# Moving the operands of a feed-forward network into an SBUF pool of their own, ahead of the others

## The chip, the core and the metric

The kernel runs on one core of a Trainium2 chip. The metric is the device time of one execution in microseconds (us). A profile of one execution gives, per instruction, its start and duration on each engine: TensorE (PE for matmuls, PEld for its weight loads), VectorE (DVE), ScalarE (ACT), GpSimd (POOL) and SyncE (SP), which issues the transfers.

## The reference

The input x is 4 x 1024 tokens of 512 features, fp32. It is layer-normalised to xn, and the output is x plus two branches of xn:

```python
# time mixing ("attention"), hidden width 704
xx  = shift_by_one_token(xn) - xn
k   = (xn + xx * time_mix_k) @ Wk.T
r   = (xn + xx * time_mix_r) @ Wr.T
state = state * w + relu(k_t)        # a scan over the tokens, w = exp(-exp(decay))
out = layernorm((state * r) @ Wv.T)
# feed-forward network (FFN), hidden width 2048
X = xn.astype(float16)
D = gelu(X.astype(float32) @ W0.T + bias0).astype(float16)
E = (D.astype(float32) @ W1.T + bias1).astype(float16)
```

## The kernel before

The tokens are worked in eight blocks of 512 (`blocks`, line 62). One pass of the loop at line 456 does for block i: the time mixing up to the gated states (`attention`), then the FFN (`ffn`), in which the other work of the block is placed between steps: `attention_out` ahead of step 0, the layer norm of the next block ahead of step 4, its transposes and mixed inputs ahead of step 7 (lines 478 to 481).

**Precision.** The products of the time mixing (lines 310, 345, 355) are fp32 matmuls, which the hardware records as two matmuls each. The FFN uses the type float32r, one matmul each; to keep its accuracy the weights are split into a high and a low part (`split`, line 115: ScalarE rounds, VectorE takes the difference), and both parts are multiplied into the same accumulator. The activations are fp16 values widened to float32r and need no split.

**The FFN.** Features lie on the 128 partitions. One step n of 16 covers 128 of the 2048 hidden units:

- *up* (`up`, lines 400 to 416): eight matmuls into one PSUM bank `pd`: for each of four feature chunks c, the stationary operand is a 128 x 128 piece of `w0h[c]` and then of `w0l[c]`, the moving operand `xf[:, c, :]` with 512 columns (line 405). ScalarE applies GELU to an fp16 tile `d16`, VectorE casts it to the float32r tile `d` (lines 413 and 415).
- *down* (`down`, lines 418 to 426): for each of four groups s of 128 tokens, the stationary operand is `d[:, s*128:(s+1)*128]`, the moving operand the high and then the low part of `w1` with 512 columns (line 420). The four accumulators `pe[s]` are kept over all 16 steps.

The up of step n + 2 is issued ahead of the down of step n (`AHEAD = 2`), so TensorE gets eight up matmuls, eight down matmuls, and so on; at the end of a block, where no up is left, the downs of steps 13, 14 and 15 follow one another, 24 in a row. In the last block those 24 are ordered by s (lines 442 to 447), so that each group of tokens can be finished early.

`w0h` and `w0l` are held in SBUF for the whole run. `w1` is too large for that: block 0 loads and splits it step by step and writes the parts to DRAM; later blocks read them back, 512 KB per step, into three buffers (`load_w1`, line 132). The two parts of the last step of the last block go to two buffers of the tag `raw` instead (lines 133 to 140).

**Where tiles lie.** `tile_pool` reserves SBUF for a pool when it is opened, pool after pool, and in a pool tag after tag in the order of first use, each tag with its number of buffers. So a tile's address follows from the sizes of all that stand ahead of it. The pools are `const` (one buffer for each name), `one`, `two`, `three` and `four` (lines 67 to 71), named after their number of buffers. `ident` (512 bytes per partition), small tables and the eight time-mixing weights of 2816 bytes stand first in `const`, so `w0h` and `w0l` begin at 896 modulo 2048 bytes, `xf`, which is in `one` behind `xnT` (8208 bytes) and others, at 992, and `w1` in `three` and `d` in `four` at 288.

Of the kernel before, what the change touches and what calls it, by code (L numbers as in the profile page):

```python
# [10 lines left out]
F32R = mybir.dt.float32r  # L11
# [3 lines left out]
P = 128  # L15
# [4 lines left out]
def time_mix_and_gelu_ffn(  # L20
# [27 lines left out]
    B, T, C = x.shape  # L48
    HID = wkT.shape[1]
    N = w0T.shape[1]  # L50
    TB = 512
    NS = TB // P
    NC = C // P
# [10 lines left out]
    def pool(name, bufs, **kw):  # L64
        return ctx.enter_context(tc.tile_pool(name=name, bufs=bufs, **kw))

    const = pool("const", 1)
    one = pool("one", 1)
    two = pool("two", 2)
    three = pool("three", 3)  # L70
    four = pool("four", 4)
# [43 lines left out]
    def split(hi, lo, raw):  # L115
        nc.scalar.copy(hi, raw)
        nc.vector.tensor_sub(lo, raw, hi.bitcast(F32))  # L117

    W0G = 512
    w0h = [const.tile([P, N], F32R, name=f"w0h_{c}") for c in range(NC)]  # L120
    w0l = [const.tile([P, N], F32R, name=f"w0l_{c}") for c in range(NC)]

    w1_dram = [dram.tile([P, 2, C], F32R, name=f"w1d_{n}") for n in range(NN)]

# [7 lines left out]
    def load_w1(i, n):  # L132
        if i == len(blocks) - 1 and n == NN - 1:

            parts = [
                three.tile([P, C], F32R, tag="raw", name=f"w1_{i}_{n}_{p}") for p in range(2)
            ]
            for p in range(2):
                nc.sync.dma_start(parts[p].bitcast(F32), w1_dram[n][:, p, :].bitcast(F32))
            return parts  # L140
        w1 = three.tile([P, 2, C], F32R, tag="w1", name=f"w1_{i}_{n}")
        if i == 0:
            raw = three.tile([P, C], F32, tag="raw", name=f"w1raw_{n}")
            nc.sync.dma_start(raw, w1T[n * P : (n + 1) * P, :])
            split(w1[:, 0, :], w1[:, 1, :], raw)
            nc.sync.dma_start(w1_dram[n].bitcast(F32), w1.bitcast(F32))
        else:
            nc.sync.dma_start(w1.bitcast(F32), w1_dram[n].bitcast(F32))
        return [w1[:, p, :] for p in range(2)]
# [128 lines left out]
        return x16s, xk  # L278

    def ffn_input(i, x16s):  # L280
        xf = one.tile([P, NC, TB], F32R, tag="xf", name=f"xf_{i}")
        for c in range(NC):
            nc.vector.tensor_copy(xf[:, c, :], x16s[c])
        return xf
# [103 lines left out]
    def finish(i, s, z, pe):  # L388
        b, t0 = blocks[i]
        e16 = two.tile([P, C], F16, tag="e16", name=f"e16_{i}_{s}")  # L390
        nc.vector.tensor_add(e16, pe, b1_sb)  # L391
        nc.vector.tensor_add(z, z, e16)  # L392
        nc.sync.dma_start(out[b, t0 + s * P : t0 + (s + 1) * P, :], z)

    def ffn(i, xf, between, state):


        pe = [ps_e.tile([P, C], F32, tag="pe", name=f"pe_{i}_{s}") for s in range(NS)]

        def up(n):  # L400
            pd = ps_mm.tile([P, TB], F32, tag="mm", name=f"pd_{i}_{n}")
            cols = slice(n * P, (n + 1) * P)
            for c in range(NC):
                for w in (w0h, w0l):
                    nc.tensor.matmul(  # L405
                        pd,
                        w[c][:, cols],
                        xf[:, c, :],
                        start=(c == 0 and w is w0h),
                        stop=(c == NC - 1 and w is w0l),  # L410
                    )
            d16 = two.tile([P, TB], F16, tag="d16", name=f"d16_{i}_{n}")
            nc.scalar.activation(d16, pd, AF.Gelu, bias=b0_sb[:, n : n + 1])  # L413
            d = four.tile([P, TB], F32R, tag="d", name=f"d_{i}_{n}")
            nc.vector.tensor_copy(d, d16)  # L415
            return d

        def down(n, s, d, w1):
            for part in range(2):
                nc.tensor.matmul(  # L420
                    pe[s],
                    d[:, s * P : (s + 1) * P],
                    w1[part],
                    start=(n == 0 and part == 0),
                    stop=(n == NN - 1 and part == 1),
                )

        last = 3 if i == len(blocks) - 1 else 0  # L430
        AHEAD = 2
        waiting = [(up(n), load_w1(i, n)) for n in range(AHEAD)]
        for n in range(NN):
            if n in between:
                between[n]()
            if n + AHEAD < NN:
                waiting.append((up(n + AHEAD), load_w1(i, n + AHEAD)))
            if n < NN - last:
                operands = waiting.pop(0)
                for s in range(NS):  # L440
                    down(n, s, *operands)
        if last:
            with tc.manual_schedule(engines={nc.tensor.engine, nc.vector.engine}):
                for s in range(NS):
                    for n, operands in zip(range(NN - last, NN), waiting):
                        down(n, s, *operands)
                    finish(i, s, state["zs"][s], pe[s])
        return pe
# [4 lines left out]
    nc.scalar.activation(w_sb, w_sb, AF.Exp)  # L453
    nc.scalar.activation(w_sb, w_sb, AF.Exp, scale=-1.0)
    xf = ffn_input(0, x16s)
    for i in range(len(blocks)):
        more = i + 1 < len(blocks)
# [25 lines left out]
        if more:  # L483
            x16s, xk = state["mixed"]
            xf = ffn_input(i + 1, x16s)
            for s in range(NS):
                finish(i, s, state["zs"][s], pe[s])
# [43 lines left out]
```

## Time and profile before

957.68 us, median of three runs (957.37 to 958.03); the profiled execution has a span of 956.5 us.

| view of the profile | what it says |
|---|---|
| TensorE clock granted | 0.998 of full on average; half speed only in the first microseconds and at the very end |
| pd matmuls, line 405 | 1024, mean duration 402 ns (with w0h) and 395 ns (with w0l) |
| pe matmuls, line 420 | 1024, mean duration 393 ns |
| weight loads of both | 188 ns each |
| fp32 matmuls, lines 310 and 345 | 960 of full size, mean 591 to 599 ns |
| GELU on ScalarE, line 413 | 128, 687 ns each |
| cast to d on VectorE, line 415 | 128, 424 ns each |
| w1 read back from DRAM | 111 transfers of 512 KB, 3.3 us from issue to landing (median) |
| DMA | 106.47 MB, 111 GB/s over the span |

A matmul's recorded duration reaches from its start to a modelled end, and the next one starts well before that end; the distance from start to start is what a matmul costs a busy TensorE. A group's line gives its merged busy time and the mean duration of one.

### The profile page before, as it was taken

What the parts mean: (1) busy time and instruction counts of PE and PEld (TensorE: products, weight loads), DVE (VectorE), ACT (ScalarE), POOL (GpSimd) and SP (SyncE); (2) the same over time, 40 slices, a digit from 0 to 9 for tenths busy, and PEclk for the clock granted to TensorE, in tenths of its full rate; (3) what the DMA queues carried; (4) which work ended last, traced back from release to release, by engine and by line L of the source; (5) the groups of instructions that cost most, each with busy time, mean ns of one, the idle gap of its engine ahead of it and who ended that gap; (6) DMA issues with size and microseconds to landing.
All of it is one profiled execution on the core that took longest, in us unless ns stands there. A gap on an engine that the chain in (4) does not pass through costs nothing.

```text
span 956.5 us, 8658 instructions
## 1 busy us (share of the span) xinstructions
PE 939.8 (98%) x3216; PEld 582.2 (61%) x3216; DVE 486.0 (51%) x836; ACT 160.5 (17%) x264; POOL 53.7 (6%) x128
## 2 busy tenths in 40 slices
PE   5999999999999999999999999999999999999998
PEld 2447764478644785458854488545884458744686
DVE  6548852385424844259343593436924279232512
ACT  5322320012100121002201021010210102101021
POOL 1001000010001000011000100001100020000100
PEclk9999999999999999999999999999999999999999
DMA  8734570045400354014530154302542023410243
GB/s 267 244 128 143 207 266 1 0 132 197 156 0 23 132 182 149 0 31 144 178 132 1 33 173 169 110 1 64 181 153 88 0 86 135 156 64 0 73 147 110
DMA packets 43368, 106.47 MB, mean 111 GB/s; under 512 B 8256, under 2 KB 8256, under 8 KB 43328
## 3 DMA queue, kind: packets, MB, share of 16 engines
q1 hardware_dynamic: 43328, 105.94, 33.0%
q8 instruction: 25, 0.41, 0.2%
q14 instruction: 15, 0.12, 0.0%
HBM read 89.14 MB, written 16.78 MB: 111 GB/s over the span
## 4 chain that ended last, share of the span: by engine, by line
PE 95%; DVE 3%; ACT 1%; DMA 0%; issue 0%; POOL 0%; SPq 0%; DVEq 0%
PE pd L405 24%; PE pe L420 23%; PE po L345 15%; PE pr L310 14%; PE pk L310 14%; PE pkr L310 3%; PE po L355 2%; DVE xnT L196 1%; DMA x<-in_L_attn_x 0%; DVE z L392 0%; DVE w L117 0%; DVE e L391 0%; DVE xk L275 0%; ACT xk L235 0%; DVE d L415 0%
## 5 line engine op out<-in xcount | busy, mean ns | idle before, releaser
L420 PE MATMUL pe<-w,d 128*128 128x512 f32 x1024 | 254.9, 393 | 0.9 <-DVE w L117 0.6
L420 PEld LDWEIGHTS pe<-w,d 128*128 128x128 f32 x1024 | 192.0, 188 | 45.1 <-DVE w L117 1.0
L405 PE MATMUL pd<-xf,w0h 128*128 128x512 f32 x512 | 205.8, 402 | 0.0
L405 PE MATMUL pd<-xf,w0l 128*128 128x512 f32 x512 | 202.0, 395 | 0.0
L413 ACT ACTIVATE d<-pd,b_sb 128x512 f16<-128x512 f32 x128 | 87.9, 687 | 428.8 <-PE pd L405 428.8
L310 PE MATMUL pk<-xk,wk 128*128 128x512 f32 x320 | 146.0, 599 | 3.1 <-DVE xk L242 3.1
L310 PE MATMUL pr<-xnT,wr 128*128 128x512 f32 x320 | 144.0, 591 | 0.0
L345 PE MATMUL po<-wv_sb,g 128*128 128x512 f32 x320 | 140.8, 595 | 0.0
L415 DVE CAST d<-d 128x512 fp32r<-128x512 f16 x128 | 54.3, 424 | 138.1 <-ACT d L413 137.2
L405 PEld LDWEIGHTS pd<-xf,w0h 128*128 128x128 f32 x512 | 96.1, 188 | 31.0 <-issue 5.9
L405 PEld LDWEIGHTS pd<-xf,w0l 128*128 128x128 f32 x512 | 96.1, 188 | 24.5 <-issue 1.9
L310 PEld LDWEIGHTS pk<-xk,wk 128*128 128x128 f32 x320 | 60.8, 191 | 78.5 <-issue 71.1
L310 PEld LDWEIGHTS pr<-xnT,wr 128*128 128x128 f32 x320 | 60.6, 189 | 76.9 <-issue 76.4
L345 PEld LDWEIGHTS po<-wv_sb,g 128*128 128x128 f32 x320 | 60.1, 190 | 75.6 <-issue 74.9
L196 DVE STREAM_TRANSPOSE xnT<-x 32x512 f32<-32x512 f32 x112 | 78.7, 703 | 2.2
L297 DVE TENSOR_TENSOR_SCAN st<-w_sb,carry,rk 128x512 f32<-128x512 f32 (+1 forms) x24 | 30.8, 1283 | 70.3 <-ACT rk L295 70.3
L295 ACT ACTIVATE rk<-pk 128x512 f32<-128x512 f32 x40 | 24.0, 601 | 233.3 <-PE pk L310 233.3
L175 DVE BATCH_NORM_STATS2 sty<-po 128x6 f32<-128x512 f32 x32 | 22.1, 689 | 72.8 <-PE po L355 67.9
L297 DVE TENSOR_TENSOR_SCAN st<-w_sb,rk 128x512 f32<-128x512 f32 (+1 forms) x24 | 29.3, 1222 | 54.9 <-ACT rk L295 54.8
L321 DVE TENSOR_TENSOR g<-st,pr 128x512 f32<-128x512 f32 x40 | 27.5, 687 | 53.7 <-PE pr L310 53.6
L169 POOL TENSOR_SCALAR ry<-mvy 128x1 f32<-128x1 f32 x32 | 11.4, 356 | 508.0 <-DVE mvy L176 508.0
L310 PE MATMUL pkr<-xnT,wr 128*64 128x512 f32 x64 | 29.2, 598 | 0.0
(56 smaller groups left out, 439.7 us busy)
## 6 DMA issues: line engine op xcount, KB each, us to landing
w<-w1d SPq DMA_DIRECT2D x111, 512.0 KB, 3.3
x<-in_L_attn_x SPq DMA_DIRECT2D x32, 256.0 KB, 4.3
xres<-in_L_attn_x SPq DMA_DIRECT2D x32, 256.0 KB, 2.7
w1d<-w SPq DMA_DIRECT2D x16, 512.0 KB, 3.3
out<-z SPq DMA_DIRECT2D x32, 256.0 KB, 4.8
w0raw<-in_L_ffn_W SPq DMA_DIRECT2D x16, 256.0 KB, 4.1
w1raw<-in_L_ffn_W SPq DMA_DIRECT2D x16, 256.0 KB, 4.0
wk<-in_L_attn_Wk SPq DMA_DIRECT2D x4, 352.0 KB, 6.2
```

The source lines that it names most:

```text
L175: nc.vector.bn_stats(st6, src)
L196: nc.vector.transpose(dst[i * Q : (i + 1) * Q, :, :, j, :], src[j * Q : (j + 1) * Q, :, :, i, :],)
L295: nc.scalar.activation(rk[:hw], pk, AF.Relu)
L297: nc.vector.tensor_tensor_scan(st[:hw], w_sb[:hw, h : h + 1].to_broadcast([hw, TB]), rk[:hw], 0.0 if t0 == 0 else carry[:hw, h : h + 1], A ...
L310: nc.tensor.matmul(dst, w[c][:, cols], src, start=(c == 0), stop=(c == NC - 1))
L321: nc.vector.tensor_mul(g[:, h, :], st, pr)
L345: nc.tensor.matmul(pos[s], g[:, h, s * P : (s + 1) * P], wv_sb[:, h, :], start=(first and h == 0), stop=(not first and h == NF - 1),)
L355: nc.tensor.matmul(pos[s], gh[rows, s // 2, :], wv_sb[rows, NF, :], start=first, stop=not first)
L405: nc.tensor.matmul(pd, w[c][:, cols], xf[:, c, :], start=(c == 0 and w is w0h), stop=(c == NC - 1 and w is w0l),)
L413: nc.scalar.activation(d16, pd, AF.Gelu, bias=b0_sb[:, n : n + 1])
L415: nc.vector.tensor_copy(d, d16)
L420: nc.tensor.matmul(pe[s], d[:, s * P : (s + 1) * P], w1[part], start=(n == 0 and part == 0), stop=(n == NN - 1 and part == 1),)
```

## The change

A pool named `wide` is opened ahead of all others. `w0h`, `w0l`, `xf`, `w1` (three buffers, as before) and `d` (four, as before) are allocated in it. All of them have buffers of 2048, 4096 or 8192 bytes per partition, so that each begins at the same offset modulo 2048.

```diff
+    wide = pool("wide", 1)
     const = pool("const", 1)
     one = pool("one", 1)
...
-    w0h = [const.tile([P, N], F32R, name=f"w0h_{c}") for c in range(NC)]
-    w0l = [const.tile([P, N], F32R, name=f"w0l_{c}") for c in range(NC)]
+    w0h = [wide.tile([P, N], F32R, name=f"w0h_{c}") for c in range(NC)]
+    w0l = [wide.tile([P, N], F32R, name=f"w0l_{c}") for c in range(NC)]
...
-        w1 = three.tile([P, 2, C], F32R, tag="w1", name=f"w1_{i}_{n}")
+        w1 = wide.tile([P, 2, C], F32R, tag="w1", name=f"w1_{i}_{n}", bufs=3)
...
-        xf = one.tile([P, NC, TB], F32R, tag="xf", name=f"xf_{i}")
+        xf = wide.tile([P, NC, TB], F32R, tag="xf", name=f"xf_{i}")
...
-            d = four.tile([P, TB], F32R, tag="d", name=f"d_{i}_{n}")
+            d = wide.tile([P, TB], F32R, tag="d", name=f"d_{i}_{n}", bufs=4)
```

The start addresses in the two built programs, modulo 2048 bytes (the pieces of one tile follow at multiples of 512 or 2048):

| tile | role | before | after |
|---|---|---|---|
| w0h, w0l | stationary, up | 896 | 128 |
| xf | moving, up | 992 | 128 |
| d | stationary, down | 288 | 128 |
| w1 | moving, down | 288 | 128 |
| raw (last step of the last block) | moving, down | 288 | 288 |
| all others (wk, wr, wv, xnT, xk, g, x, z, ...) | | as listed by the pools | the same offsets as before |

## The prediction

> **What bounds the kernel now.** I read the page from the top: busy shares, the chain of waits, the groups, and then, because a busy TensorE says little by itself, the timeline of single matmuls. The first two (busy line, then the chain by engine and by line):
>
> ```profile
> PE 939.8 (98%) x3216; PEld 582.2 (61%) x3216; DVE 486.0 (51%) x836; ACT 160.5 (17%) x264; POOL 53.7 (6%) x128
> ...
> PE 95%; DVE 3%; ACT 1%; DMA 0%; issue 0%; POOL 0%; SPq 0%; DVEq 0%
> PE pd L405 24%; PE pe L420 23%; PE po L345 15%; PE pr L310 14%; PE pk L310 14%; PE pkr L310 3%; PE po L355 2%; DVE xnT L196 1%; DMA x<-in_L_attn_x 0%; DVE z L392 0%; DVE w L117 0%; DVE e L391 0%; DVE xk L275 0%; ACT xk L235 0%; DVE d L415 0%
> ```
>
> TensorE carries 95% of the chain; the FFN's two products (pd and pe) are 47% of the span. Does it wait? All waits of TensorE:
>
> ```profile
> PE pt L223 <- DVE x L179: 8.3, 1, 8.3
> PE pk L310 <- DVE xk L242: 3.1, 2, 2.7
> PE pe L420 <- DVE w L117: 0.6, 1, 0.6
> PE pe L420 <- DVE d L415: 0.3, 1, 0.3
> ```
>
> 12.3 us in all, 11.4 of them at the start. So the time is the sum of the spacings between matmul starts, and only those can change it. The timeline of TensorE in block 2 (start, merged duration, group):
>
> ```profile
> 354.99 2.01 PE L420 MATMUL pe<-w,d 128*128 128x512 f32 x8
> 356.84 0.39 PE L405 MATMUL pd<-xf,w0h 128*128 128x512 f32 x1
> ...
> 358.70 2.01 PE L420 MATMUL pe<-w,d 128*128 128x512 f32 x8
> ...
> 362.41 5.65 PE L420 MATMUL pe<-w,d 128*128 128x512 f32 x24
> 367.90 2.31 PE L310 MATMUL pk<-xk,wk 128*128 128x512 f32 x5
> ```
>
> Eight pe take 356.84 - 354.99 = 1.85 us (231 ns each), eight pd 1.86 us (232.5 ns). Durations near 393 ns overlap and are not the rate. The last line pair is the important one: at a block's end there is no pd left and 24 pe stand in a row, 5.49 us, 229 ns each. Within that row the spacing settles. Its weight loads from the eleventh or so on, and a row of pd ahead of the attention output, where 16 pd stand together:
>
> ```profile
> 364.95 2.68 PEld L420 LDWEIGHTS pe<-w,d 128*128 128x128 f32 x12
> ```
>
> ```profile
> 290.98 0.39 PE L405 MATMUL pd<-xf,w0l 128*128 128x512 f32 x1
> ...
> 292.38 0.39 PE L405 MATMUL pd<-xf,w0l 128*128 128x512 f32 x1
> ```
>
> Twelve loads in 2.68 us, the last one 0.19 us long: (2.68 - 0.19) / 11 = 226.4 ns. From the 1 ns start times behind this view the settled pe spacing is 226, 227, 227 and again, 226.67 on average, in all eight blocks, from about the eleventh matmul on. The pd never get there: six intervals in 292.38 - 290.98 = 1.40 us are 233.3 ns, and the starts behind it read 238, 231, 231 (or 237, 231, 232) over and over. Settled, the same instruction on the same shapes costs 226.7 ns in pe and 233.3 ns in pd. In the eight-by-eight alternation that fills a block neither settles: pe repeats 229, 229, 233, 236, 224, 231, 236, 232. Over the kernel, leaving out the gaps over 300 ns, 1000 pd gaps average 232.46 ns and 1012 pe gaps 230.69 ns.
>
> **Why two rates: the addresses.** The products are alike in type, width and weight size. In pe the moving w1 starts at 288 modulo 2048 and the stationary d at 288 plus a multiple of 512: their distance is 0 modulo 512. In pd the moving xf starts at 992, the stationary w0 at 896 plus a multiple of 512: the distance is 416 modulo 512. Within pd four different w0 offsets (384, 896, 1408, 1920 modulo 2048) give one pattern, and within pe the four d offsets give one settled rate, so multiples of 512 don't matter here. The accumulation bank doesn't either: in the last block six pe in a row go to one bank, elsewhere two, and both settle at 226.67. What is left is how the stream of moving data and the weight load of the next matmul, which starts 3 ns after each matmul, lie to each other in SBUF. This is inferred from two configurations only; distance and absolute offset are not separated by the trace.
>
> **What the Trainium skill says.** "TensorE: Matmul & The Clock Gate", section "Step-by-step: what each phase is for": TensorE has two independent SBUF read ports, and loading the next weights doesn't steal bandwidth from the running matmul. The trace does not bear that out for this type: the fp32 products, where the load has time to spare, run at 429 ns for two passes, 214.5 a pass, and the one-pass products at 227 to 233. The same page, "Back-to-back issue gap", gives N/2.4 + 2.5, an estimate of 215.8 ns for 512 columns: the fp32 pass agrees, the FFN is 11 to 17 ns above it. "SBUF — State Buffer", "Specifications (TRN2)", gives 16-byte lines with a penalty on crossing. A 512-byte weight row has 32 of them, and 226.67 - 213.3 is 32 cycles at 2.4 GHz, 233.3 - 213.3 is 48: an estimate that fits, no more. The section "Operand start alignment" there speaks of legality and says that nothing was timed.
>
> **The change part by part.** *Instructions.* None is added, removed or moved: each engine's list, with its waits, is the same in both kernels, so no new wait and no new queueing. Cost 0, not even hidden work. *The other tiles.* The new pool is 94,208 bytes, 46 times 2048, so what stays behind it (wk, wr, wv, xnT, xk, g, x, d16, z) keeps its offset modulo 2048. I cost the attention's 1,152 fp32 matmuls and all of VectorE and ScalarE at nothing: same offset, and the other engines lie beside TensorE in any case. *The up product.* xf moves from 992 to 128, w0 from 896 to 128: distance 0 modulo 512. *The down product.* w1 and d both go from 288 to 128: distance unchanged. Also the change from one product to the other, every eight matmuls, now keeps the distance (before: weights 288 under xf 992, weights 896 under w1 288), so a settled stream need not be upset nearly 30 times a block.
>
> If distance decides, all settle at 226.67:
> - pd: 1000 x (232.46 - 226.67) = 5.8 us
> - pe: 1012 x (230.69 - 226.67) = 4.1 us
> - given back, settling: a stream that starts anew takes some ten matmuls. In the last block, after a 338 ns gap, 229, 233, 236, 224, 231, 236, 228, 233, 231 add up to 41 ns over the settled rate. Two new starts a block (after the attention, after its output) and one more in the last: 17 x 0.041 = 0.7 us.
> - given back, the last w1: its two parts lie in the pool of the raw loads, still at 288, against a d at 128. 24 matmuls in the last block alternate with it; at 4 ns each 0.1 us.
> - given back, block 0: its pe wait for the w1 split on VectorE (0.6 us above). The 168 FFN matmuls ahead of that wait would save about 168 x 4.9 ns = 0.8 us, which can be lost in it: between 0 and 0.8, taken as 0.4 since some of the loads may be early.
>
> Sum 9.9 - 0.7 - 0.1 - 0.4 = 8.7 us: 957.7 - 8.7 = 949.0 us. Faster TensorE makes no other engine the bound: a step of 16 matmuls shrinks from 3.71 to 3.63 us, while its w1 transfer lands in 3.3 us with three buffers, and one GELU (687 ns) and one cast (424 ns) are two steps ahead.
>
> **Rivals.**
> - *Absolute offset decides, the other way.* w0 is the operand on a multiple of 128 now, and pd is the slower product. If weights on such a border are what costs, pe joins pd at 233.3: 1000 x 0.87 + 1012 x 2.64 = 3.5 us, 961.2 us. For it: only two configurations are seen. Against: four w0 and four d offsets made no difference.
> - *The alternation never settles.* The pattern may come from the switching of products (a new accumulation, its semaphore), not from addresses. Then pd looks like pe now: 1000 x (232.46 - 231) = 1.5 us, 956.2 us; or nothing moves, 957.7. Against: the 24 pe in a row switch operands and accumulators too and stay settled.
> - *A clean border removes the whole overhead.* 128 is a multiple of 128 and 288 isn't. At the fp32 pass rate: 1000 x 17.96 + 1012 x 16.19 = 34 us, 923 us. Nothing seen runs so, with the load under a one-pass matmul.
>
> **Chances.** Distance decides 0.64; never settles or no change 0.12; absolute offset, slower 0.17; whole overhead gone 0.07. Faster by over 0.2% is 0.64 + 0.07 = 0.71, within 0.2% is 0.12, slower 0.17. The range: the first case with its unknowns (block 0 and settling, 947.8 to 950) widened to 945 for a rate a few ns better, and up to 959 over the no-change case and the near half of the slower one.
>
> **What would show it.** Right: pd and pe both at 226.67 away from new starts, eight of each in 1.81 us instead of 1.86 and 1.85; mean matmul durations of both groups near 389 to 390; fp32 rows at 592 as now; the same four waits of TensorE. Wrong: settled pd at 233, or a settled pe that is no longer 226.67 (then the absolute offset counts), or a longer wait for the w1 split in block 0 that eats the gain.

## The result, and the profile after

The changed kernel takes 949.54 us (median of six runs, 949.0 to 950.27) against 957.61 us for the kernel before in the same session (957.27 to 958.03): a ratio of 0.9916, 95% interval 0.9903 to 0.9928, or 8.1 us less. The two profiled executions lie further apart, 956.5 and 947.2 us: 0.9 us of that is TensorE's first wait, for x, which was 8.3 and 7.4 us long in them (7.2 to 8.5 us in the profiles of this document).

The busy line of the changed kernel's page and its chain by engine:

```profile
PE 931.0 (98%) x3216; PEld 583.0 (62%) x3216; DVE 485.7 (51%) x836; ACT 160.5 (17%) x264; POOL 53.7 (6%) x128
...
PE 93%; DVE 4%; ACT 1%; issue 1%; DMA 0%; POOL 0%; DVEq 0%
```

TensorE is as full as before and its busy time is 8.8 us shorter with the same 3216 instructions; no other engine's busy time moved by more than 0.8 us. All waits of TensorE in the changed kernel:

```profile
PE pt L226 <- DVE x L182: 7.4, 1, 7.4
PE pk L313 <- DVE xk L245: 3.1, 2, 2.8
PE pe L423 <- DVE w L120: 0.8, 1, 0.8
PE pe L423 <- DVE d L418: 0.6, 2, 0.3
```

The same four lines; the two in front of pe grew from 0.9 to 1.4 us. The wait for w stands in block 0 in both kernels. The one wait for d of before stands in the last block and is still there; the second, 0.30 us, is new and stands in block 0 as well. The timeline of TensorE in block 2 (start, merged duration, group), at the place that was shown of before:

```profile
351.49 1.98 PE L423 MATMUL pe<-w,d 128*128 128x512 f32 x8
353.30 0.39 PE L408 MATMUL pd<-xf,w0h 128*128 128x512 f32 x1
...
355.11 1.98 PE L423 MATMUL pe<-w,d 128*128 128x512 f32 x8
...
358.74 5.60 PE L423 MATMUL pe<-w,d 128*128 128x512 f32 x24
364.18 3.17 PE L313 MATMUL pk<-xk,wk 128*128 128x512 f32 x7
```

Eight pe take 353.30 - 351.49 = 1.81 us and eight pd 355.11 - 353.30 = 1.81 us (before 1.85 and 1.86), 226.7 ns each by the 1 ns start times behind this view. The row of 24 takes 5.44 us instead of 5.49, 226.7 ns from its first matmul on. In the starts the alternation reads 226, 227, 227 in pd, in pe, and across every switch.

What is left shows after a new start. The first pd after block 2's attention, in the same view:

```profile
286.99 0.40 PE L408 MATMUL pd<-xf,w0l 128*128 128x512 f32 x1
...
289.31 0.39 PE L408 MATMUL pd<-xf,w0l 128*128 128x512 f32 x1
289.54 0.39 PE L408 MATMUL pd<-xf,w0h 128*128 128x512 f32 x1
...
290.45 4.02 PE L348 MATMUL po<-wv_sb,g 128*128 128x512 f32 x9
```

Ten intervals in 289.31 - 286.99 = 2.32 us are 232 ns each; the next four read 226, 227, 227 and 226 in the starts. Before, this row stayed at 233.

The sum over the kernel, from the starts (gaps over 300 ns left out again; a gap counts for the product it starts in, up to the next FFN matmul):

| | before, ns | after, ns | us |
|---|---|---|---|
| pd, 1000 gaps (999 after) | 232.46 | 227.43 | -5.0 |
| pe, 1012 gaps | 230.69 | 226.87 | -3.9 |
| gaps over 300 ns of block 0's FFN, beyond what ordinary gaps take | | | +0.75 |
| all fp32 matmuls | 463.84 us | 463.80 us | 0.0 |

-8.9 + 0.75 is -8.15 us; the medians differ by 8.1.

### The profile page after: what moved, and what is told of

Its sections match the earlier page's. It is cut to its first block, busy times and chain, and to the rows that moved or that the text cites. A ratio compares the mean times of both kernels' runs of the same rounds, so it can differ in the third digit from the quotient of the medians.

```text
span 947.2 us, 8658 instructions
## 1 busy us (share of the span) xinstructions
PE 931.0 (98%) x3216; PEld 583.0 (62%) x3216; DVE 485.7 (51%) x836; ACT 160.5 (17%) x264; POOL 53.7 (6%) x128
## 4 chain that ended last, share of the span: by engine, by line
PE 93%; DVE 4%; ACT 1%; issue 1%; DMA 0%; POOL 0%; DVEq 0%
PE pd L408 23%; PE pe L423 22%; PE po L348 15%; PE pr L313 15%; PE pk L313 14%; PE pkr L313 3%; PE po L358 2%; DVE xnT L199 1%; DVE w L120 1%; DVE stx L178 0%; DVE d L418 0%; DMA x<-in_L_attn_x 0%; DVE z L395 0%; DVE e L394 0%; DVE xk L278 0%
## 5 line engine op out<-in xcount | busy, mean ns | idle before, releaser
L423 PE MATMUL pe<-w,d 128*128 128x512 f32 x1024 | 251.2, 390 | 1.4 <-DVE w L120 0.8
L408 PE MATMUL pd<-xf,w0l 128*128 128x512 f32 x512 | 199.9, 390 | 0.0
```

The lines of the kernel that those rows point to most:

```text
L408: nc.tensor.matmul(pd, w[c][:, cols], xf[:, c, :], start=(c == 0 and w is w0h), stop=(c == NC - 1 and w is w0l),)
L423: nc.tensor.matmul(pe[s], d[:, s * P : (s + 1) * P], w1[part], start=(n == 0 and part == 0), stop=(n == NN - 1 and part == 1),)
```

## The experiments

The distance theory was that the settled spacing of float32r matmuls depends on the distance between moving operand and weights. Its rivals were that the absolute offset decides, and that the switch from one product to the other does, wherever the operands lie.

### Distances and offsets by themselves

```diff
+    for r, (m, d) in enumerate(runs):            # 45 pairs (moving offset, distance), bytes
+        m, w = m // 4, (4096 + m + d) // 4
...
+        for k in range(REP):      # 64
+            nc.tensor.matmul(q, big[:, w : w + P], big[:, m : m + 512], ...)
```

> The kernel leaves the model out altogether: 45 rows of 64 float32r matmuls (128 x 128 weights, 512 columns) on one tile, each row with its own offset of the moving operand and its own distance to the weights; the output is not the reference's. Rows a to aa..bf: moving operand at a multiple of 2048 bytes, distance 0, 16, 32, ... 496 bytes beyond 4096; then distances 512, 1024, 1536, 4 and 8; then distance 0 with both operands moved by 16, 32, 64, 160, 256, 288; then distance 416 with both moved by 32 and 96. Distance theory: distance 0 settles at 226.7 ns, also when both are moved and at 512, 1024 and 1536; distance 416 settles at 233.3 ns, also when both are moved; other distances lie between or beyond. Absolute-offset theory: the rows with both operands moved differ from the row at the same distance by several ns. If switching of products and not addresses made the difference, all 45 rows settle alike.

(By the kernel's own comment `big` begins at a multiple of 512 bytes; that it is one of 2048, as the text says, is not shown. No distance depends on it.)

Some rows of its timeline (start, merged duration; a row's 64 matmuls cost the difference between its start and the next row's). qab is distance 16, qac 32, qad 48; qaq 256, qar 272, qas 288, qat 304:

```profile
22.71 14.68 PE L70 MATMUL qab<-big 128*128 128x512 f32 x64
37.23 15.09 PE L70 MATMUL qac<-big 128*128 128x512 f32 x64
52.15 15.09 PE L70 MATMUL qad<-big 128*128 128x512 f32 x64
...
245.24 14.67 PE L70 MATMUL qaq<-big 128*128 128x512 f32 x64
259.75 14.68 PE L70 MATMUL qar<-big 128*128 128x512 f32 x64
274.26 15.09 PE L70 MATMUL qas<-big 128*128 128x512 f32 x64
289.19 15.09 PE L70 MATMUL qat<-big 128*128 128x512 f32 x64
```

14.52 us at 16, 14.92 at 32; 14.51 at 256 and 272, 14.93 at 288: the pattern returns after 256 bytes. Settled spacings (second half of each row):

| distance, bytes | ns | distance, bytes | ns |
|---|---|---|---|
| 0 | 226.7 | 128 | 233.5 |
| 16 | 226.7 | 144 | 233.5 |
| 32 | 233.4 | 160 | 233.4 |
| 48 | 233.3 | 176 | 230.0 |
| 64 | 233.2 | 192 | 228.9 |
| 80 | 232.0 | 208 | 231.9 |
| 96 | 234.3 | 224 | 233.3 |
| 112 | 233.3 | 240 | 226.7 |

The rows 256 to 496 repeat these within 0.1 ns, and 512, 1024 and 1536 give 226.7. With both operands moved by 32, 64, 160, 256 or 288 bytes distance 0 stays at 226.7, and 416 stays at 233.3 when both are moved by 32 or 96. So with the moving operand on a 32-byte border and distances in steps of 16 bytes, the distance modulo 256 decides, and 226.7 ns is the least that any distance gave. Distances 4 and 8 cost 232.5 and 230.6. Off the border the rule fails: with both operands moved by 16, distance 0 costs 231.1. All FFN tiles of these kernels begin at multiples of 32.

### All operands together, elsewhere

```diff
     wide = pool("wide", 1)
+    shift = wide.tile([P, 40], F32, name="shift")    # 160 bytes ahead; another pool behind
+    nc.vector.memset(shift, 0.0)                     # keeps the other tiles where they were
...
```

> All FFN operands together at 288 modulo 2048 instead of 128, all other tiles where they were. Distance theory: as the changed kernel, 949.5 us within 0.5, all float32r matmuls settled at 226.7 ns. Absolute-offset theory: w0 leaves its multiple of 128 bytes, so the time differs from 949.5 us by more than 1 us, in either direction.

949.36 us, 0.9908 of before (0.9895 to 0.9922). The average spacings are 227.04 ns in pd and 226.72 in pe: the multiple of 128 has no part in the settled rate. Both are a little under the changed kernel's. The last w1, which stays at 288, agrees with the rest here. And the first pd after the attention settle sooner: from block 1 on after four gaps (236, 228, 234, 230 in block 2, 21 ns over the settled rate together), where the changed kernel takes ten and 60 ns. So a new start depends on more than the distance, here by some 0.4 us over the kernel; on what is not known.

### The old distance at the new place

```diff
...
-        xf = wide.tile([P, NC, TB], F32R, tag="xf", name=f"xf_{i}")
+        xf = late.tile([P, NC, TB], F32R, tag="xf", name=f"xf_{i}")   # behind the other four and 96 bytes
```

> The changed kernel with only xf moved on by 96 bytes (224 against weights at 128), which is the old distance of the up product, 416 modulo 512, at the new place; all other tiles keep their offsets. Distance theory: pd settles at 233.3 ns again, pe is disturbed again by each switch, 957 to 958 us. Absolute-offset theory (weights and w1 stay where they are): 949.5 us.

959.1 us, 1.0012 of before (1.0006 to 1.0019): moving one tile by 96 bytes takes all of the gain away, and 1 us more than I had expected. The first groups of its page answer to those of the changed kernel, which follow:

```profile
L430 PE MATMUL pe<-w,d 128*128 128x512 f32 x1024 | 254.3, 393 | 1.0 <-DVE w L123 0.6 <-DVE d L425 0.3
L415 PE MATMUL pd<-xf,w0h 128*128 128x512 f32 x512 | 207.6, 406 | 0.0
L415 PE MATMUL pd<-xf,w0l 128*128 128x512 f32 x512 | 202.8, 396 | 0.0
```

```profile
L423 PE MATMUL pe<-w,d 128*128 128x512 f32 x1024 | 251.2, 390 | 1.4 <-DVE w L120 0.8 <-DVE d L418 0.6
L408 PE MATMUL pd<-xf,w0h 128*128 128x512 f32 x512 | 203.8, 398 | 0.0
L408 PE MATMUL pd<-xf,w0l 128*128 128x512 f32 x512 | 199.9, 390 | 0.0
```

pe is slower too (254.3 us merged against 251.2), though its own operands didn't move. The starts show where: in block 2 an eight of pe reads 231, 231, 236, 229, 231, 231, 227, 227, and the row of 24 settles at 226.67 from its seventh gap on. The average spacings are 234.31 ns in pd, above the 232.46 of before, and 230.04 in pe. In the row of 16 pd of block 2 they settle near 233 as before; in the alternation single gaps reach 235 to 241 and eight pd take 1.88 us, which the settled rate doesn't give. 1000 x 1.85 ns more in pd less 1012 x 0.65 in pe is 1.2 us, which is about the extra microsecond. Why pd fares worse here than in the kernel before was not found.

### One product at a time

```diff
-        w1 = wide.tile([P, 2, C], F32R, tag="w1", name=f"w1_{i}_{n}", bufs=3)
+        w1 = three.tile([P, 2, C], F32R, tag="w1", name=f"w1_{i}_{n}")
-            d = wide.tile([P, TB], F32R, tag="d", name=f"d_{i}_{n}", bufs=4)
+            d = four.tile([P, TB], F32R, tag="d", name=f"d_{i}_{n}")
```

> One part of the change alone: w0 and xf together in the first pool at 128, w1 and d left in their old pools at 288. Distance is 0 within each product, but 160 or 352 at every switch between them. If a switch disturbs the stream, as the pe of the kernel before suggest, both products keep a spacing near 230.7 ns: 1000 x (232.46 - 230.7) = 1.8 us, 955.8 us. If only the distance within a product counts: 949.5 us.

956.68 us, 0.9986 of before (0.9979 to 0.9992). Both products are at distance 0 now, and yet only 1.4 us of 8.1 come. Block 2's alternation and last row in its timeline:

```profile
354.20 2.01 PE L423 MATMUL pe<-w,d 128*128 128x512 f32 x8
357.90 2.01 PE L423 MATMUL pe<-w,d 128*128 128x512 f32 x8
361.60 5.64 PE L423 MATMUL pe<-w,d 128*128 128x512 f32 x24
367.07 3.17 PE L313 MATMUL pk<-xk,wk 128*128 128x512 f32 x7
```

A step of 16 takes 3.70 us, 231.2 ns a matmul, where the changed kernel takes 3.62; the last row takes 5.47. The averages are 231.90 in pd and 230.03 in pe. After each switch between 128 and 288 the stream settles anew, and eight matmuls hardly suffice: pe reads 231, 231, 236, 228, 232, 231, 227, 228, pd 236, 233, 236, 224, 231, 236, 228, 232. Most of the change's gain is therefore that *all five* tiles agree, not that either product does.

### The two products 256 bytes apart

```diff
+    gap = pool("gap", 1)      # 256 bytes
+    late = pool("late", 1)    # w1 and d: at 384 modulo 2048, w0 and xf stay at 128
...
```

> The changed kernel with w1 and d at 384 modulo 2048 and w0 and xf at 128, all other tiles where they are: distance 0 within a product, 256 at each switch. If 256 is the period, as the sweep says, the switch disturbs nothing: 949.5 us within 0.5, pd and pe settled at 226.7 ns. If the period were 512 at a switch: as with the up operands alone together, 955 to 957 us.

949.55 us, 0.9915 of before (0.9902 to 0.9929); pd 227.46 and pe 226.89 ns. The changed kernel, run beside it, gave 949.43 us (0.9913, 0.99 to 0.9927), pd 227.44 and pe 226.86.

> The changed kernel itself on this chip, for comparison with the two others: 949.5 us within 0.5.

So the period of 256 bytes holds at the switches too, and a common offset modulo 2048 is more than is needed.

### Whose weights count

```diff
+            m, w = pair[k % 2][0] // 4, (4096 + pair[k % 2][1]) // 4    # two kinds in turn
+            nc.tensor.matmul(q, big[:, w : w + P], big[:, m : m + 512], ...)
```

> The model is left out; nine rows of 64 float32r matmuls, two kinds in turn, the output is not the reference's. Row aa: both kinds at distance 0. Row ab: moving at 0, weights at 160. Rows ac, ae, ag: kind A has moving and weights at 0, kind B both at 64, 96 or 160, so that each matmul lies at distance 0 from its own weights and at 64, 96 or 160 from the weights that are loaded under it. Rows ad, af, ah: A moving 0 and weights 64, 96 or 160, B the other way round, so that the distance to the own weights is 64, 96 or 160 and to those loaded under it 0. Row ai: as ac with 256. If the load under the stream decides, ad, af, ah and ai settle at 226.7 ns and ac, ae, ag at 231 to 235. If the distance to the own weights decides, ac, ae and ag settle at 226.7 and ad, af and ah do not. aa 226.7 and ab 233.3 as in the sweep.

The two rows with 96 bytes, and the start of the next:

```profile
67.36 15.13 PE L71 MATMUL qae<-big 128*128 128x512 f32 x64
82.33 14.89 PE L71 MATMUL qaf<-big 128*128 128x512 f32 x64
97.06 15.13 PE L71 MATMUL qag<-big 128*128 128x512 f32 x64
```

qae takes 14.97 us and qaf 14.73, where a row at distance 0 took 14.52 in the sweep. qaa and qai settle at 226.7 ns and qab at 233.3. With 64, 96 and 160 the rows with the own weights at 0 (ac, ae, ag) give 231.7, 234.0 and 234.0, those with the weights loaded under the stream at 0 (ad, af, ah) 231.7, 230.0 and 230.0. The load under the stream would account for the first three (231 to 235 was expected) but not for the others, which were to settle at 226.7; the distance to the own weights would account for the others alone. So neither expectation holds as a whole: being right in one relation isn't enough. In all six rows the moving operand alternates as well, which may count by itself. Which of the three relations costs how much stays open; that all of them at 0 modulo 256 give the least is what the case needs.

### What the spacing is made of

```diff
+    runs = [(big, 4, wc, 512, d) for d in (0, 160) for wc in (128, 96, 64, 32)]   # weight columns
+    runs += [(big, 4, 128, mc, d) for d in (0, 160) for mc in (480, 384, 256)]    # moving columns
+    runs += [(full, 4, 128, 512, d) for d in (0, 160)]                            # fp32
+    runs += [(half, 2, 128, 512, d) for d in (0, 16, 32, 64, 96, 128, 160, 192, 224)]   # fp16
```

> The model is left out again: 25 rows of 64 matmuls from one tile, the output is not the reference's. Rows aa..ad and ae..ah: float32r with 128, 96, 64 and 32 weight columns, 512 moving columns, at distance 0 and at 160. Rows ai..ak and al..an: 128 weight columns, 480, 384 and 256 moving columns, at distance 0 and 160. Rows ao and ap: fp32 at 0 and 160. Rows aq..ay: fp16 at distance 0, 16, 32, 64, 96, 128, 160, 192, 224. If the weight load takes cycles from the stream, one for each 16 bytes of weights at distance 0 and one and a half at 160, then 128, 96, 64, 32 columns cost 226.7, 223.3, 220.0, 216.7 ns at distance 0 and 233.3, 228.3, 223.3, 218.3 at 160, and with 256 moving columns 120 and 126.7 ns. If instead the load has a fixed latency of some 227 ns that the next matmul waits for, the spacing doesn't fall with the moving columns, and falls to the stream's 213.3 as soon as the load is shorter. fp32, where a pass has time to spare: 429 ns at both distances. fp16: 215 ns or a little over, with less difference than float32r, since both streams are half as many bytes.

Rows of its timeline: float32r with 64 weight columns at distance 0 (qac, 14.71 us; a row with 128 took 14.52 in the sweep), 384 and 256 moving columns at distance 0 (qaj, qak), 256 at 160 (qan), fp16 at 0 and 160 (qaq, qaw):

```profile
37.38 14.87 PE L77 MATMUL qac<-big 128*64 128x512 f32 x64
52.09 14.99 PE L77 MATMUL qad<-big 128*32 128x512 f32 x64
...
140.26 11.28 PE L77 MATMUL qaj<-big 128*128 128x384 f32 x64
151.38 7.83 PE L77 MATMUL qak<-big 128*128 128x256 f32 x64
159.04 14.23 PE L77 MATMUL qal<-big 128*128 128x480 f32 x64
...
184.42 7.83 PE L77 MATMUL qan<-big 128*128 128x256 f32 x64
192.09 55.10 PE L77 MATMUL qao<-full 128*128 128x512 f32 x128
...
301.96 13.98 PE L77 MATMUL qaq<-half 128*128 128x512 f16 x64
315.77 13.98 PE L77 MATMUL qar<-half 128*128 128x512 f16 x64
...
384.84 13.98 PE L77 MATMUL qaw<-half 128*128 128x512 f16 x64
398.65 13.98 PE L77 MATMUL qax<-half 128*128 128x512 f16 x64
```

The idea that each 16 bytes of weights takes a cycle from the stream falls: at distance 0, 96, 64 and 32 weight columns settle at 230.0, 229.7 and 231.7 ns, dearer than 128 columns at 226.7. A fixed latency of 227 ns for the load falls as well: 384 and 256 moving columns settle at 173.3 and 120.0 ns. From 256 to 384 and from 384 to 512 columns the spacing grows by 53.3 ns for 128 columns, so a column costs 1/2.4 ns (512 take 213.3 ns), and what is left at each of these three lengths is 13.3 ns a matmul. 480 columns don't lie on that line: at 216.7 ns, 16.7 are left. The price of a bad distance comes on top. It shrinks with the length, 6.7 ns with 512 moving columns, 3.3 with 480 (220.0 against 216.7) and with 384 (176.7 against 173.3), none with 256. It is also smaller with narrower weights: 96, 64 and 32 weight columns settle at 231.2, 231.0 and 233.3 ns at distance 160, 1.2 to 1.6 ns more than at 0. fp32 gives 429.2 a record at both distances, fp16 215.8 at all nine: of the three types only float32r minds.

### The last step of the last block

```diff
-                three.tile([P, C], F32R, tag="raw", name=f"w1_{i}_{n}_{p}") for p in range(2)
+                wide.tile([P, C], F32R, tag="raw", name=f"w1_{i}_{n}_{p}", bufs=3) for p in range(2)
```

(and the other two tiles of the tag `raw`)

> The changed kernel with the raw buffers in the new pool as well, so that the last step of the last block also reads its w1 at 128. The last 24 matmuls settle at 226.7 ns; 0.1 to 0.2 us less than the changed kernel, which the times can't tell from nothing.

949.49 us (0.9913 of before, 0.99 to 0.9927), against the changed kernel's 949.43. The saving can't be read from the times, but the starts show the effect: after the last stall the row reads 231, 231, 236, 228, 233, 230 and then 227, where the changed kernel goes on between 224 and 238 to the end.

## Why the prediction was right

- **The bound.** TensorE's spacing set the time: its gaps account for the whole difference, and beyond block 0 no engine is in the chain that wasn't there before.
- **The two settled rates.** 226.67 and 233.3 ns were read from two rows in the trace of before and taken for two distances. The sweep gives 226.7 and 233.4 at these distances and shows that the absolute offset, which the trace could not exclude, has no part in the settled rate among the offsets that pools give. What the step had too coarse is the period: 256 bytes, not 512 (416 is the same as 160). And it took the weights loaded under the stream for the partner; the rows in pairs show that this relation at 0 alone doesn't settle. That neither touches the number is owed to the change, which puts all five tiles at one offset, and not to the reasoning; in this the forecast was lucky.
- **The switches.** The step said that a stream that keeps its distance across switches need not be upset. With each product at distance 0 but the two apart, 1.4 us came; with all together, 8.1. Of the steps this is the one that carries the gain. The rival that the alternation never settles would have given 956.2 or 957.7 us; it is refuted for equal offsets. So are the slower rival (961.2 us) and the one in which a clean border frees the whole overhead (923 us): at 128 the rate settles at 226.7 and nowhere below. The stated range, 945 to 959 us, held the never-settling rival too; the eights of 1.81 us decide between them, not the range.
- **The gross sum.** 9.9 us was the most if all settled. Left over the settled rate are 1000 x 0.76 + 1012 x 0.20 ns = 1.0 us, where 0.7 for new starts and 0.1 for the last w1 were taken. The new starts are a little dearer than the one I read (240, 235, 233, 236, 224, 231, 236, 228, 233, 231 is 60 ns over the settled rate, not 41). The first matmuls of the new starts, up to 794 ns long as recorded, also keep the mean duration of the w0h group at 398 ns, where 389 to 390 was named; its median is 389.
- **Block 0.** 0.4 us was taken between 0 and 0.8; it is 0.75. The pe that waits for the w1 split starts 105.86 us after TensorE's first matmul, before 105.99: the split comes nearly when it came, so what TensorE saves ahead of it turns into waiting. VectorE sets that time: its norm, transposes, mixed inputs and splits make up nearly all of the chain from 77.2 to 113.2 us (before from 93.1 to 114.3). So the step's sentence that a faster TensorE makes no other engine the bound doesn't hold in this stretch, while this term had allowed for it. These two terms, 0.2 and 0.35 us too small, are the 0.6 us between the 8.7 us forecast and the 8.1 measured.
- **Nothing else moved.** fp32 matmuls 463.8 us in both.
- **The estimate of lines**, made from the 16-byte lines that the Trainium skill gives ("SBUF — State Buffer", "Specifications (TRN2)"), fitted two numbers and was wrong as a mechanism, as the narrower weights show. No step of the sum used it.
- **The two ports.** The Trainium skill ("TensorE: Matmul & The Clock Gate", "Step-by-step: what each phase is for") says that loading the next weights takes no read bandwidth from the running matmul. fp32 and fp16 agree, in that their spacing (429.2 and 215.8 ns) doesn't depend on the distance. For float32r with 384 columns or more it does; whether the load takes bandwidth there is not shown. Nor is it shown that an fp32 record is two passes, as the prediction has it: that is read from 429.2 being close to twice 213.3. And the page gives N/2.4 + 2.5 ("Back-to-back issue gap") for a matmul by itself; the stream of fp16 matmuls here, at 215.8 ns, agrees with it.

What physically costs the 6.7 ns of a bad distance, and the 13.3 ns of every float32r matmul, was not found.

## What to carry to other kernels

Where TensorE is full with float32r matmuls of 128 weight columns and 384 to 512 moving columns, place every operand of the stream, moving and stationary and of all products that alternate, at one offset modulo 256 bytes, a multiple of 32; it costs no instruction and here gave 0.84%. Getting one product right is worth little if the stream switches to operands elsewhere every few matmuls, and fp16 streams (nine distances) and fp32 streams (two) showed no such effect. Look for it by taking start-to-start spacings in the longest unbroken rows of each product: two settled rates for the same shape pointed to addresses here.

## What was not expected of the hardware

- The spacing has a memory: after a disturbance three to ten matmuls run at 223 to 240 ns before the rate settles at a good distance. At most bad distances it never comes to one value but cycles (238, 231, 231 at 160).
- Narrower weights are slower at distance 0: 230.0 ns with 96 columns and 231.7 with 32, against 226.7 with 128.
- At 512, 384 and 256 moving columns a float32r matmul at distance 0 costs 13.3 ns over its columns at 2.4 per ns, at 480 it costs 16.7; an fp16 one of 512 columns costs 2.5 ns over them (215.8 against 213.3).
- With 256 moving columns the distance no longer matters on average (120.0 ns both), though at 160 the single gaps go from 116 to 125.
